# Layer 0's two projections of five chunks by two-by-two blocks with seven products

## The chip, the core and the metric

The kernel runs on one core of a Trainium2 chip. The time is the device time of one execution, in microseconds (us). The engines are TensorE (PE in the profile; PEld are its weight loads), VectorE (DVE), ScalarE (ACT), GpSimd (POOL) and SyncE (SP, here only a queue that issues DMAs). All data are float32. One f32 matmul instruction of the program appears in the profile as two passes, so "x32" in a row of PE means 16 matmuls of the program.

## What is computed

There are 16 sequences of 256 tokens with 256 features, 4096 tokens in all. Layer 0 is a linear recurrence that is gated by a two-layer MLP; layer 1 is causal attention with low-rank keys and values, gated by a linear layer with low-rank experts. Only layer 0 is touched:

```
x  = L0_attn_x
xn = layernorm(x)
s  = recurrence(xn)            # complex diagonal state of 32, plus D * xn
h  = gelu(xn @ proj1.T + b1)   # 256 -> 1024
g  = silu(h @ proj2.T + b2)    # 1024 -> 256
x  = x + s * g
# then layer 1 on x
```

## The kernel before, in words

The tokens are taken in 8 chunks of 512 (two sequences). The program is one list of instructions for each engine. PE's list is the order of the program: a small class, InOrder (line 40), chains each instruction to the one before it. The lists v0 (DVE), a0 (ACT) and g0 (POOL) are chained in the same way where they are used; operations written with nc.vector, nc.scalar or nc.gpsimd are placed by the scheduler. A second class, Later (line 64), keeps instructions back and writes them in portions.

For a chunk of layer 0 the steps are these. norm0 makes layer-norm statistics on DVE (four bn_stats), the power −1/2 on POOL (rs) and the scaled tokens xn on DVE. turn0 turns xn by 8 PE transposes (tp) and copies them out of PSUM to xnT, the first half on ACT, the second on DVE (line 199). hidden (line 655) is the first projection: 8 blocks of 128 hidden rows, each of 2 matmuls with N=512 (rows "ph<-xnT,p1T"), then a GELU on ACT (line 665) into hT. recur (line 680) is the recurrence: 4 matmuls (pb), on DVE a product v and four products w with PSUM operands, on POOL v+w (line 694), on DVE a scan (696), again four products w and hs (699), on POOL the last subtraction (700). mix (line 703), called twice, is the second projection: 256 tokens each time, 16 matmuls with N=256 (rows "pf<-p2T,hT"), a DVE sum with the bias (713) and a Silu on ACT (715). direct (718) is dx = xn * D, two POOL operations (723). outs (726) is four small matmuls (py) and two DVE sums (739). finish0 (741) multiplies by the gate and adds to x, two POOL operations a half.

The chunks 0 and 1 are interleaved by hand at the start, while weights arrive and DVE builds the tables of the recurrence (rot, ct, stb, sns, decay) by doubling columns. In chunks 0 to 3 fold_heads (623) loads and multiplies layer 1's query and output weights of four heads each (psq and pso, four loads on SP, lines 629 to 632), for layer 1. In the last chunk the first steps of layer 1 (norm_begin, transpose_chunk, kv_begin with the row pkv, query_mm) are interleaved. PSUM has three pools: four banks for ph, pb, psq, pso and tp, used in turn as a ring, two for py and two for pf.

Of the kernel before, what the change touches and what calls it, by code (L numbers as in the profile page):

```python
# [18 lines left out]
P = 128  # L19
B, S, D = 16, 256, 256  # L20
NTOK = B * S
CH = 512
# [19 lines left out]
def tile_two_layers(ctx: ExitStack, tc: tile.TileContext, d: dict, out: bass.AP):  # L42
# [192 lines left out]
    def norm_begin(ch):  # L235
        k = chunks[ch]
        st = sm1.tile([P, TPC, 6], F32, tag="ln_st", name=f"st_1_{ch}")
        k.mv = sm1.tile([P, TPC, 2], F32, tag="ln_mv", name=f"mv_1_{ch}")
        v = sm1.tile([P, TPC], F32, tag="ln_ve", name=f"ve_1_{ch}")
        k.rs = sm1.tile([P, TPC], F32, tag="ln_rs", name=f"rs_1_{ch}")  # L240
        for j in range(TPC):
            ve.bn_stats(st[:, j, :], X[ch][:, j, :])
        for j in range(TPC):
            ve.bn_aggr(k.mv[:, j, :], st[:, j, :])
        ve.tensor_scalar(v, k.mv[:, :, 1], LN_EPS, None, ALU.add)
        gp.tensor_tensor(k.rs, v, mhalf, ALU.pow)
# [182 lines left out]
    with ExitStack() as l0:  # L429
# [4 lines left out]
        ps_mm = l0.enter_context(tc.tile_pool(name="ps_mm", bufs=4, space=PSUM))  # L434
        ps_y = l0.enter_context(tc.tile_pool(name="ps_y", bufs=2, space=PSUM))
        ps_f = l0.enter_context(tc.tile_pool(name="ps_f", bufs=2, space=PSUM))
# [186 lines left out]
        def fold_heads(g):  # L623
            hs = slice(g * HG, (g + 1) * HG)
            big = qp.tile([P, 2, HG, D], F32, tag="qg", name=f"wqn_wo{g}")
            small = qm.tile([P, 2, HG, KVL], F32, tag="qmul", name=f"wkb_wvb{g}")
            wqn, wo, wkb, wvb = big[:, 0], big[:, 1], small[:, 0], small[:, 1]

            nc.sync.dma_start(wqn, d["wq_nopeT"][hs].rearrange("h p e -> p h e"))
            nc.sync.dma_start(wkb, d["wkb_T"][:, hs, :])  # L630
            nc.sync.dma_start(wvb, d["wvb_T"][:, hs, :])
            nc.sync.dma_start(
                wo, d["Wo"][g * HG * P : (g + 1) * HG * P, :].rearrange("(h p) e -> p h e", p=P)
            )
            psq = ps_mm.tile([P, 2, HG // 2, 2, KVL], F32, tag="mm", name=f"psq{g}")
            for h in range(HG):
                for c in range(2):
                    pe.matmul(
                        psq[:, c, h // 2, h % 2, :], wqn[:, h, c * P : (c + 1) * P],
                        wkb[:, h, :], start=True, stop=True,  # L640
                    )
            prs = slice(g * HG // 2, (g + 1) * HG // 2)
            nc.vector.tensor_copy(
                wlat[:, :, hs, :], psq.rearrange("p c a b f -> p c (a b) f")
            )
            pso = ps_mm.tile([P, HG // 2, D], F32, tag="mm", name=f"pso{g}")
            for h in range(HG):
                pe.matmul(
                    pso[64 * (h % 2) : 64 * (h % 2) + 64, h // 2, :], wvb[:, h, :],
                    wo[:, h, :], start=True, stop=True,  # L650
                )
            nc.scalar.copy(wout[:, prs, :], pso)


        def hidden(ch, xnT):
            hT = []
            for fc in range(NFC):
                ph = ps_mm.tile([P, CH], F32, tag="mm", name=f"ph_{ch}_{fc}")
                for c in range(2):
# [5 lines left out]
                (a0 if ch == 1 else nc.scalar).activation(  # L665
                    ht, ph, AF.Gelu, bias=b1[:, fc : fc + 1]
                )
# [12 lines left out]
        def recur(ch, xnT):  # L680

            pb = ps_mm.tile([P, S], F32, tag="mm", name=f"pb_{ch}")
            for c in range(2):
                for b in range(2):
                    pe.matmul(
                        pb[64 * b : 64 * b + 64, :], bT[:, c, :],
                        xnT[:, c, b * S : (b + 1) * S], start=(c == 0), stop=(c == 1),
                    )

# [4 lines left out]
            nc.gpsimd.tensor_tensor(v, v, w, ALU.add)  # L694
            g = a2.tile([P, S], F32, tag="g", name=f"g_{ch}")
            nc.vector.tensor_tensor_scan(g, decay, v, 0.0, ALU.mult, ALU.add)
            swapped(w, g)
            h = a2.tile([P, S], F32, tag="hs", name=f"hs_{ch}")
            nc.vector.tensor_tensor(h, g, ct, ALU.mult)
            nc.gpsimd.tensor_tensor(h, h, w, ALU.subtract)  # L700
            return h

        def mix(ch, jp, hT):
            pf = ps_f.tile([P, 2, D], F32, tag="pf", name=f"pf_{ch}_{jp}")
            for j2 in range(2):
                cols = slice((2 * jp + j2) * P, (2 * jp + j2 + 1) * P)
                for fc in range(NFC):
                    pe.matmul(
                        pf[:, j2, :], hT[fc][:, cols], p2T[:, fc, :],
                        start=(fc == 0), stop=(fc == NFC - 1),  # L710
                    )
            zf = a2.tile([P, 2, D], F32, tag="zf", name=f"zf_{ch}_{jp}", bufs=3)
            nc.vector.tensor_tensor(zf, pf, bc(b2_bc, 2), ALU.add)
            if ch:
# [3 lines left out]
        def direct(ch, xn, g=nc.gpsimd):  # L718

            dx = []  # L720
            for b in range(2):
                dx.append(a2.tile([P, 2, D], F32, tag="dx", name=f"dx_{ch}_{b}", bufs=4))
                g.tensor_tensor(dx[b], xn[:, 2 * b : 2 * b + 2, :], bc(d_bc, 2), ALU.mult)
            return dx

        def outs(ch, h, dx):

            py = [
                ps_y.tile([P, 2, D], F32, tag="py", name=f"py_{ch}_{b}") for b in range(2)
# [8 lines left out]
            for b in range(2):  # L738
                nc.vector.tensor_tensor(dx[b], py[b], dx[b], ALU.add)

        def finish0(ch, jp, dx, zf):
            js = slice(2 * jp, 2 * jp + 2)
            nc.gpsimd.tensor_tensor(dx[jp], dx[jp], zf, ALU.mult)
            nc.gpsimd.tensor_tensor(X[ch][:, js, :], X[ch][:, js, :], dx[jp], ALU.add)
# [81 lines left out]
        for ch in range(NCH):  # L826
            last = ch == NCH - 1
            if last:
                place.update(pool=ps_mm, tag="mm")
                norm_begin(0)  # L830
                norm_end(0)
                norm_begin(1)
            if ch > 1:
                hT = hidden(ch, xnT)
            if last:
                transpose_chunk(0)
            if ch == 0:

                zf = [mix(ch, jp, hT) for jp in range(2)]
                turn_b()  # L840
                dx0 = direct(0, xn, g0)
                xn3 = norm0(2)
                hT = hidden(1, xnT2)
                for z in zf:
                    a0.activation(z, z, AF.Silu)
                g = recur(ch, xnT)
                fold_heads(ch)
                h0, zf0 = g, zf
            else:
                if ch == 1:  # L850
                    xn2 = xn3
                elif ch + 1 < NCH:
                    xn2 = norm0(ch + 1)
                g = recur(ch, xnT)
                if ch < NH // HG:
                    fold_heads(ch)
                if ch == 1:
                    zf = mix(ch, 0, hT)
                    outs(0, h0, dx0)
                    for jp in range(2):  # L860
                        finish0(0, jp, dx0, zf0[jp])
                if ch + 1 < NCH:
                    xnT2 = turn0(ch + 1, xn2)
                if last:
                    kv_begin(0)
                    norm_end(1)
                if ch > 1:
                    zf = mix(ch, 0, hT)
                if last:
                    kv_end(0)  # L870
                    router_chunk(0)
                    key_chunk(0)
                if ch == 1:
                    zf = [zf, mix(ch, 1, hT)]
                    dx = direct(ch, xn)
                    outs(ch, g, dx)
                    for jp in range(2):
                        finish0(ch, jp, dx, zf[jp])
                else:
                    dx = direct(ch, xn)  # L880
                    outs(ch, g, dx)
                    if last:
                        query_mm(0, 0)
                        query_mul(0, 0)
                        query_mm(0, 1)
                        query_mul(0, 1)
                        query_rot(0)
                        query_move(0)
                    finish0(ch, 0, dx, zf)
                    zf = mix(ch, 1, hT)  # L890
                    if last:
                        ve.tensor_scalar(bb_bc, bb_bc, 0.5, None, ALU.mult)
                        query_mm(0, 2)
                        query_lat(0, 2)
                        query_mm(0, 3)
                        query_lat(0, 3)
                        query_mm(1, 0)
                        query_mul(1, 0)
                        query_mm(1, 1)
                        query_mul(1, 1)  # L900
                        query_rot(1)
                        query_mm(1, 2)
                        query_lat(1, 2)
                    finish0(ch, 1, dx, zf)
            xn, xnT = xn2, xnT2
# [372 lines left out]
```

## Time and profile before

| what | value |
|---|---|
| median of 3 runs | 946.45 us (945.7 to 947.52) |
| the profiled execution | 946.5 us, of it 944.7 us span |
| mean granted PE clock | 0.998 |
| ph, first projection | 288 passes, 114.2 us in rows |
| pf, second projection | 512 passes, 113.6 us in rows |
| layer 0 | about the first 260 us |

A row "A us, mean ns" gives the busy time of a group of like instructions and the mean of one; the two names before and after "<-" are the target and its sources, and the shapes are partitions x elements. Rows of pipelined matmuls overlap, so the mean of one is longer than the distance from start to start. A chain row names the work, or the wait, that held the end back. In the timeline a row stands for one or several like instructions in a row, with start and duration.

### The profile page before, as it was taken

The page shows a single profiled execution, that of the slowest core. Times are in us where ns is not written, and L with a number is a line of the kernel's source. Part 1 is how long each engine was busy: PE and PEld are TensorE (multiplying, and loading weights), DVE is VectorE, ACT ScalarE, POOL GpSimd, SP SyncE. Part 2 cuts the span into 40 slices and gives each one's busy share as a digit, 9 for nine tenths or more (in the row PEclk, how much of TensorE's full clock was granted, in tenths as well). Part 3 has the DMA queues.
Part 4 walks back from the last instruction along what each step waited for, and adds up shares of the span by engine and source line. Part 5 has one row for each costly group of instructions (what it writes and reads, how often), then busy time and mean ns, then how long its engine had stood idle before and what let it go on. Part 6 is the DMA issues. An engine that isn't in the chain of part 4 may idle for free.

```text
span 944.7 us, 15757 instructions
## 1 busy us (share of the span) xinstructions
PE 928.2 (98%) x4778; PEld 667.7 (71%) x4778; DVE 617.1 (65%) x1943; ACT 427.4 (45%) x1421; POOL 419.0 (44%) x760
## 2 busy tenths in 40 slices
PE   8999999999999899999999999999999999999988
PEld 7765766676676666777677777767777776777776
DVE  6884541343166688867967876796787679677662
ACT  3323223323335646545544564554465455446550
POOL 1327313332145454554554555445464544546450
PEclk9999999999999999999999999999999999999999
DMA  9630000000013777776787777678676767867870
GB/s 282 216 112 1 1 1 0 1 1 1 0 20 60 200 194 188 205 201 172 184 194 187 189 175 206 176 176 208 167 195 170 215 174 171 213 167 186 230 201 29
DMA packets 196597, 133.90 MB, mean 142 GB/s; under 512 B 142304, under 2 KB 187168, under 8 KB 196512
## 3 DMA queue, kind: packets, MB, share of 16 engines
q1 hardware_dynamic: 194192, 128.68, 52.3%
q0 software_dynamic: 1344, 3.67, 1.1%
q8 instruction: 39, 0.64, 0.3%
q10 hardware_dynamic: 976, 0.53, 0.2%
q14 instruction: 46, 0.38, 0.1%
HBM read 63.11 MB, written 52.95 MB: 123 GB/s over the span
## 4 chain that ended last, share of the span: by engine, by line
PE 86%; DVE 7%; POOL 2%; DMA 1%; ACT 1%; SPq 1%; issue 1%; POOLq 0%; ACTq 0%
PE pq L53 22%; PE sc L53 14%; PE po L53 11%; PE ph L53 10%; PE av L53 9%; PE pf L53 9%; PE pg L53 4%; PE pm L53 1%; PE pkv L53 1%; PE tp L53 1%; POOL pr L53 1%; SPq L53 1%; DVE w L53 1%; DMA qg<-qrot 1%; DVE rot L53 1%
## 5 line engine op out<-in xcount | busy, mean ns | idle before, releaser
L53 ACT ACTIVATE pr<-sc,nm 128x256 f32<-128x256 f32 (+7 forms) x512 | 190.0, 381 | 278.5 <-DVE sr L53 196.6
L53 POOL TENSOR_SCALAR pr<-pr,sr 128x256 f32<-128x256 f32 (+7 forms) x512 | 192.6, 395 | 274.6 <-DVE sr L53 256.6
L53 PEld LDWEIGHTS sc<-kT,qg 128*128 128x128 f32 x1024 | 159.5, 191 | 62.7 <-issue 40.3
L53 PE MATMUL sc<-kT,qg 128*128 128x256 f32 (+7 forms) x1024 | 176.5, 306 | 4.9 <-DMA qg<-qrot 3.0
L53 DVE STREAM_TRANSPOSE turned<-pr 128x512 f32<-128x512 f32 x186 | 123.3, 688 | 15.2 <-POOL pr L53 14.4
L53 DVE TENSOR_REDUCE nm<-sc 128x1 f32<-128x256 f32 (+7 forms) x512 | 127.7, 301 | 6.6
L53 PE MATMUL pq<-xnT,wlat 128*128 128x512 f32 x256 | 123.6, 606 | 0.0
L53 PE MATMUL pq<-xnT,wrope 128*128 128x512 f32 x256 | 120.2, 593 | 0.0
L53 PE MATMUL po<-wout,attT 128*128 128x256 f32 x512 | 115.8, 380 | 0.0
L53 PE MATMUL ph<-xnT,p1T 128*128 128x512 f32 (+1 forms) x288 | 114.2, 555 | 1.1 <-DVE xnT L53 0.8
L53 PE MATMUL pf<-p2T,hT 128*128 128x256 f32 x512 | 113.6, 380 | 0.0
L53 PEld LDWEIGHTS po<-wout,attT 128*128 128x128 f32 x512 | 96.4, 190 | 20.9 <-issue 6.4
L53 PEld LDWEIGHTS pf<-p2T,hT 128*128 128x128 f32 x512 | 96.2, 190 | 15.0 <-issue 2.2
L53 ACT ACTIVATION_READ_ACCUMULATOR pr<-sc,nm 128x1 f32 x512 | 103.6, 202 | 0.0
L53 PEld LDWEIGHTS ph<-xnT,p1T 128*128 128x128 f32 x288 | 55.9, 195 | 54.9 <-issue 48.6
L53 PE MATMUL av<-pT,row 128*64 128x256 f32 (+1 forms) x1024 | 90.3, 329 | 0.0
L53 POOL TENSOR_TENSOR qrot<-qmul,qmul 128x512 f32<-128x512 f32 x64 | 82.6, 1311 | 10.4 <-DVE qmul L53 7.0
L53 DVE TENSOR_TENSOR qmul<-pq,rot_q 128x512 f32<-128x512 f32 x128 | 80.9, 674 | 4.9 <-PE pq L53 4.9
L53 DVE TENSOR_TENSOR sc<-sc,kmask 128x96 f32<-128x96 f32 (+1 forms) x192 | 46.0, 240 | 52.2 <-PE sc L53 50.8
L53 PEld LDWEIGHTS av<-pT,row 128*64 128x64 f32 x1024 | 64.0, 137 | 22.6 <-issue 0.5
L53 ACT ACTIVATE qg<-pq 64x512 f32<-64x512 f32 x128 | 75.5, 590 | 4.9 <-PE pq L53 4.1
L53 PEld LDWEIGHTS pq<-xnT,wlat 128*128 128x128 f32 x256 | 46.3, 193 | 32.2 <-issue 32.1
(164 smaller groups left out, 902.9 us busy)
## 6 DMA issues: line engine op xcount, KB each, us to landing
far<-turned SPq DMA_DIRECT2D x248, 192.0 KB, 3.7
pT<-far SPq DMA_DIRECT2D x62, 768.0 KB, 4.7
qg<-qrot SPq DMA_DIRECT2D x256, 64.0 KB, 2.3
x<-in_x_dram SPq DMA_DIRECT2D x7, 512.0 KB, 9.4
out_dram<-o POOLq DMA_DIRECT2D x28, 128.0 KB, 3.3
wqn_wo<-in_wq_nopeT_dram SPq DMA_DIRECT2D x4, 512.0 KB, 4.5
wqn_wo<-in_Wo_dram SPq DMA_DIRECT2D x4, 512.0 KB, 5.3
p2T<-in_proj2T_dram SPq DMA_DIRECT2D x2, 512.0 KB, 7.3
```

Source lines behind the costliest of these rows:

```text
L53: r = getattr(self.engine, name)(*args, **kw)
```

## The change

Chunks 2 to 6 compute both projections by two-by-two blocks with seven block products in place of eight. Chunks 0, 1 and 7 keep the plain method. For a product C = A·B cut into 2x2 blocks, five sums of blocks of the weights, five of the tokens, and sums of the products are needed instead:

- fast_weights1 (five POOL operations of 128x512) and fast_weights2 (four of 128x512 and one of 128x128) make the weight sums once, behind direct of chunks 0 and 1 in POOL's list and ahead of the power of norm0(2).
- fast_tokens makes the five token sums of a chunk on DVE, each 128x256 from two SBUF operands.
- A chunk is done in two steps t, each with half of the hidden rows. hid_a, hid_c and hid_e are the seven products of the first projection, into three PSUM banks r1, r2, r3 with one buffer each; c4 is a copy on ACT, f two DVE sums; a10 and a01 are GELUs from PSUM, a11 and a00 are DVE subtractions from f followed by GELUs (each GELU as two halves of 256).
- sums and sum4 (four POOL operations of 128x512 a step) add the GELU results; out_a, out_b, out_c are the seven products of the second projection of the step before, with N=128, into banks f0 to f3. zf_early, zf_mid, zf_late and zf_last add them, on DVE and (zf_late) on POOL.
- middle writes out the lists of all engines. recur is split: recur_in, and recur_out with a hook between hs and the last subtraction, in which POOL does sum4, finish0 of the second half of two chunks back and the two operations of direct.
- PSUM is given out bank by bank (Ring) in place of three pools.
- mix runs over the hidden blocks outside and the token blocks inside. The second mix of chunk 1 is written in portions into chunk 2 as filler.
- In the last chunk the plain hidden(7) is interleaved with out_a, out_b and out_c of the last step; the loads of fold_heads are issued earlier for groups 2 and 3.

The core of the diff:

```diff
-        ps_mm = l0.enter_context(tc.tile_pool(name="ps_mm", bufs=4, space=PSUM))
-        ps_y = l0.enter_context(tc.tile_pool(name="ps_y", bufs=2, space=PSUM))
-        ps_f = l0.enter_context(tc.tile_pool(name="ps_f", bufs=2, space=PSUM))
+        banks = l0.enter_context(tc.tile_pool(name="ps0", bufs=1, space=PSUM))
...
+        ps_mm = Ring("r1", "r2", "r3", "x")
+        ps_y = Ring("f2", "f3")
+        ps_f = Ring("f0", "f1")
...
+        def recur_out(ch, v, w, ve, ge, between=None):
+
+            ge.tensor_tensor(v, v, w, ALU.add)
             g = a2.tile([P, S], F32, tag="g", name=f"g_{ch}")
-            nc.vector.tensor_tensor_scan(g, decay, v, 0.0, ALU.mult, ALU.add)
+            ve.tensor_tensor_scan(g, decay, v, 0.0, ALU.mult, ALU.add)
             swapped(w, g)
             h = a2.tile([P, S], F32, tag="hs", name=f"hs_{ch}")
-            nc.vector.tensor_tensor(h, g, ct, ALU.mult)
-            nc.gpsimd.tensor_tensor(h, h, w, ALU.subtract)
+            ve.tensor_tensor(h, g, ct, ALU.mult)
+            if between:
+                between()
+            ge.tensor_tensor(h, h, w, ALU.subtract)
...
+        def fast_weights1():
...
+            g.tensor_tensor(fw.w[1], a1(0, 0), a1(1, 1), ALU.add)
+            g.tensor_tensor(fw.w[5], a1(0, 0), a1(0, 1), ALU.add)
+            g.tensor_tensor(fw.w[2], a1(1, 0), a1(1, 1), ALU.add)
+            g.tensor_tensor(fw.w[6], a1(0, 0), a1(1, 0), ALU.subtract)
+            g.tensor_tensor(fw.w[7], a1(1, 1), a1(0, 1), ALU.subtract)
...
+        def fast_tokens(xnT, which):
...
+            for m in which:
+                v0.tensor_tensor(fw.x[m], *how[m])
...
+        def hid_a(t, xnT):
...
+            hid(q, q.r[1], 4, True)
+            hid(q, q.r[0], 3, True)
+            hid(q, q.r[2], 1, True)
...
+            a0.copy(c4, q.r[1])
+            v0.tensor_tensor(fw.f, q.r[0], c4, ALU.add)
+            v0.tensor_tensor(fw.f, fw.f, q.r[2], ALU.add)
...
+        def hid_e(t):
...
+            for n, key in ((1, (1, 1)), (0, (0, 0))):
+                v0.tensor_tensor(q.a[key], fw.f, q.r[n], ALU.subtract)
+                gelu(q, key[1], q.a[key], q.a[key])
...
+        def sums(t):
...
+            g0.tensor_tensor(q.s[1], a[1, 0], a[1, 1], ALU.add)
+            g0.tensor_tensor(a[1, 0], a[0, 0], a[1, 0], ALU.subtract)
+            q.s[3] = a[1, 0]
+            g0.tensor_tensor(q.s[2], q.s[1], a[0, 0], ALU.subtract)
...
+        def middle(ch, xn, xnT, xn2, fill, out1):
...
+            if prev:
+                sums(t - 1)
+            hid_a(t, xnT)
+            out_a(t - 1) if prev else fill.write(8)
+            v, w = recur_in(ch, recur_mm(ch, xnT, X_RING))
+            hid_c(t)
+            out_b(t - 1) if prev else fill.write(4)
+
+            def rest():
+                if prev:
+                    sum4(t - 1)
+                    finish0(ch - 2, 1, out1.dx, out1.z[1], g0)
+                fw.dx[ch] = direct(ch, xn, g0)
+
+            h = recur_out(ch, v, w, v0, g0, rest)
...
+            turn_half(0)
+            hid_e(t)
+            if prev:
+                o = zf_early(ch - 1)
+                out_c(t - 1)
...
+            turn_half(1)
+            if prev:
+                zf_mid(ch - 1, o)
...
+            t += 1
+            if prev:
+                zf_late(ch - 1, o, g0)
+            sums(t - 1)
+            hid_a(t, xnT)
+            if prev:
+                zf_last(ch - 1, o)
+            for z in o.z:
+                a0.activation(z, z, AF.Silu)
+            out_a(t - 1)
...
+            if ch < NCH - 2:
+                fast_tokens(xnT2, (4, 3, 1))
+            outs(ch, h, [dx[:, 2 * b : 2 * b + 2, :] for b in range(2)], v0, XF_RING)
+            hid_c(t)
+            out_b(t - 1)
+            sum4(t - 1)
...
+        dx, dx1 = direct(0, xn, g0), direct(1, xn2, g0)
+        fast_weights1()
+        fast_weights2()
+        xn3 = norm0(2)
+        hT = hidden(1, xnT2, [])
...
+        g = recur(0, xnT)
+        fold_heads(0)
...
+        h1 = recur(1, xnT2)
+        fold_heads(1)
+        xnT = turn0(2, xn3)
+        out1 = Out()
+        out1.z = [mix(1, 0, hT)]
```

## The prediction

> **What bounds the kernel now.** I read the head of the page first, then the chain of waits over layer 0, the timeline of one chunk on VectorE (DVE) and GpSimd (POOL), and the table by stage.
>
> ```profile
> span 944.7 us, 15757 instructions
> PE 928.2 (98%) x4778; PEld 667.7 (71%) x4778; DVE 617.1 (65%) x1943; ACT 427.4 (45%) x1421; POOL 419.0 (44%) x760
> ...
> PE 86%; DVE 7%; POOL 2%; DMA 1%; ACT 1%; SPq 1%; issue 1%; POOLq 0%; ACTq 0%
> ...
> L53 PE MATMUL pf<-p2T,hT 128*128 128x256 f32 x512 | 113.6, 380 | 0.0
> ```
> TensorE (PE) is busy for 98% and is 86% of the chain. The pf row (second projection) never waits: less PE work there is worth its full time, if nothing else becomes late. In chunks 2 to 7 the chain is PE alone:
>
> ```profile
> 178.52 13.73 PE ph L53 x32
> ...
> 194.29 6.91 PE pf L53 x32
> ...
> 202.26 7.10 PE pf L53 x32
> 209.37 13.73 PE ph L53 x32
> ```
> A chunk's period is 209.37 − 178.52 = 30.85 us (33.8 with fold_heads): ph 13.73, pf 14.0, the rest pb, py and transposes. Per pass that is 13.73/32 = 0.429 us at N=512 and 6.91/32 = 0.216 at N=256.
>
> Second, how DVE and POOL share. This is the stretch at the start in which POOL multiplies dx while DVE builds rotation tables from columns of one element:
>
> ```profile
> 30.11 2.50 POOL L53 TENSOR_TENSOR dx<-xn,d_bc 128x512 f32<-128x512 f32 x2
> 30.19 1.21 DVE L53 SCALAR_TENSOR_TENSOR rot<-rot,u 128x1 f32<-128x1 f32 x1
> ...
> 31.44 1.18 DVE L53 TENSOR_TENSOR u<-rot 128x1 f32<-128x1 f32 x1
> ...
> 32.56 2.51 POOL L723 TENSOR_TENSOR dx<-xn,d_bc 128x512 f32<-128x512 f32 x2
> ...
> 32.66 1.20 DVE L53 SCALAR_TENSOR_TENSOR f<-rot,u 128x1 f32<-128x1 f32 x1
> ...
> 35.13 0.16 DVE L53 TENSOR_TENSOR u<-rot 128x1 f32<-128x1 f32 x1
> 35.32 0.22 DVE L53 SCALAR_TENSOR_TENSOR rot<-rot,u 128x1 f32<-128x1 f32 x1
> ```
> Beside POOL's products an operation on one element lasts 1.2 us; when POOL has stopped, at 35.07, it lasts 0.16 to 0.22. DVE gets about one such operation in per POOL operation. POOL can wait too: of two operations of 1.27 each when alone, these two took 2.95, with DVE's two-input g taking 0.89:
>
> ```profile
> 378.31 2.95 POOL L53 TENSOR_TENSOR qrot<-qmul,qmul 128x512 f32<-128x512 f32 x2
> ...
> 379.24 0.89 DVE L53 SCALAR_TENSOR_TENSOR g<-g,h 128x512 f32<-128x512 f32 x1
> ```
> DVE rows that read PSUM, and bn_stats, keep their length beside POOL. The recurrence in a chunk of before runs with POOL idle:
>
> ```profile
> 196.31 0.69 DVE L696 TENSOR_TENSOR_SCAN g<-decay,v 128x256 f32<-128x256 f32 x1
> 197.04 1.71 DVE L53 TENSOR_TENSOR w<-g,sns 32x256 f32<-32x256 f32 x4
> 198.76 0.42 DVE L699 TENSOR_TENSOR hs<-g,ct 128x256 f32<-128x256 f32 x1
> ```
> Last, the price of a PE gap, in the table by stage (busy us of PE, PEld, DVE, ACT and POOL, then granted clock):
>
> ```profile
> 316.00:325.00 9.00, 6.00 (x14) 3.21 (x14) 5.27 (x15) 3.94 (x17) 5.41 (x10) 0.81 0.82 203
> ```
> PE stood 3.16 us and was then granted half its clock for 3.41 us, which costs 1.7. Gaps of 1.7 (355.0) and 2.0 us (909.6) left the clock whole.
>
> **Less PE work.** Chunks 2 to 6 replace 16 block products per projection by 14 half-size ones (seven in each of two steps). First projection: 14 groups of 4 passes at N=256, 14 × 4 × 0.2157 = 12.08, against 13.73: −1.65. Second: 14 groups of 8 passes at N=128. Half of 0.216 would be 0.108; pkv, the nearest row, has 0.112 from start to start (1.87 for 16 with the entry, 0.117). So 14 × 0.893 = 12.51 (13.1 at 0.117) against 13.82: −1.31 (bound −0.7). Together −2.95 a chunk, −14.75 in five. More short groups alternate, at about 0.02 us each: +1.2 in all. Free of waits a chunk takes about 28.1.
>
> **What the other engines take on.** Per chunk POOL goes from 10 us to about 22.3 (14 operations of 128x512 at 1.27, 4 of 128x256 at 0.73, pow 1.02), DVE from 11 to 21, ACT from 10 to 14. None fills 28 us, so on average all of it lies beside PE. Order and the shared access decide.
>
> **Even step of a chunk (3 to 6).** Time from hid_a's first matmul, per-group times as above. hid_a ends 2.6, out_a 5.3, pb 6.4, then hid_c, out_b, half the transposes, hid_e, out_c, the other half: PE is through at 14.5. The next step's hid_a writes bank r2, which has one buffer now; it is free when DVE has made a11 = f − r2. In DVE's written list a11 stands behind scan, four w and hs. recur_in ends at 8.75 (from pb, PSUM operands), POOL's v+w at 9.5. In POOL's list `between` follows directly: sum4, two finish0, two dx, five operations of 128x512 with their inputs ready. DVE's scan, w ×4 and hs all have two SBUF inputs. What I must price is how they pass each other. No row has two-input operations of this size against five POOL operations in a row; the nearest is the first stretch above, one DVE operation per POOL operation. At that, six DVE operations against five of POOL: 5 × 1.16 (what POOL holds of its 1.25) + 0.55 (scan) + 5 × 0.28 = 7.75, so hs ends at 9.53 + 7.75, about 17.4 with its entries, and a11 at 18.1. PE waits 18.1 − 14.5 = 3.6. Bounds: without sharing, 0.69 + 1.71 + 0.42 = 2.8 us, a11 at 12.9, no wait; with all five first, 9.5 + 6.3 + 2.8 + 0.7 = 19.3, a wait of 4.8. I take 3.6, since the near row shows the alternation.
>
> Here a rule of the Trainium skill is weighed: "SBUF — State Buffer", section "Who interferes with whom", says that the port pair of DVE and GpSimd is an exclusive lock, held for the whole instruction, and that a DVE instruction with two SBUF inputs contends with a GpSimd one that reads SBUF. It speaks against this change, which puts most of its additions there. By the rule alone 128x512 and 128x1 operations wait alike and the step stalls 3.6. The qrot row is milder: g lost about 0.2 and POOL 0.45, 0.65 per meeting instead of about 1.2. At 0.65 × 5 the chain ends at 9.5 + 2.8 + 3.3 = 15.6, a11 at 16.3, and the wait is 1.8. But there the engines met once, not five times in a row with all of POOL's inputs ready, so I keep the first value, and 1.8 as the mild case.
>
> **Odd step.** PE work 13.55. sums, zf_late, sum4 and finish0 lie on POOL, fast_tokens (2.1) and xn on DVE, each with PE work of over 2 us between it and its reader. The a01 gelu stands behind two silus and two table loads (2 × 1.28 + 2 × 0.63) and delays hid_e by about 0.5; xn and fast_tokens may push recur_in by up to 1.3. Chunk: 14.54 + 3.65 + 13.55 = 31.74, plus 0.5 to 1.8: 32.2 to 33.5, and a third of 1.7 for a cold clock. Against 30.85 that is +1.4 to +3.2, taken as +2.2: +9 for four chunks (3 to 6). At the mild wait of 1.8: about −0.2 a chunk.
>
> **Chunk 2** has no previous halves to add and plain fillers: −2.6.
>
> **Start.** fast_weights1 and 2 (9 operations of 128x512, one of 128x128) go into POOL's list behind both direct (to 35.07) and ahead of rs_2. They run to 35.0 + 9 × 1.25 = about 46.4. DVE's table chain is then at the same rate as in the first stretch: some 18 operations in 11.4 us, worth 2.7 at 0.15 each, a loss of 8.7. In before DVE runs from the tables through xn (54.48 to 55.86) and recur_in(0) (57.9) without a gap but the 1.1 for rs. So w of pb0 ends at 66.6. psq1 needs pb0's bank (fifth tile in a ring of four): PE, at 59.1, waits till about 66.7; queued behind it stand pso1, turn0(2) and pf. The gap is above 3.16, so half a clock follows (1.7). recur_in(1) comes at 72.3, where the second half of turn0(2) needs pb1's bank; pf(1,0) starts near 73.0 instead of 63.3: **+9.7**. Bounds: 0 if the small operations slip between POOL's (the first row argues against that), 13 if each of DVE's later two-input operations waits too. Weight sums are used only at 90 and later; nobody waits for them.
>
> **Tail.** In chunk 7 the copies of xnT_0 stand on ACT behind z6's table load and two silus; pkv waits about 2.4: +2.4 (0 to 4). SP's DMA issues of fold_load 2 and 3 come earlier in the program; they wait for the buffers of groups 0 and 1 with nothing urgent behind them on SP, and are read 20 us later: nothing. The gelus that out_a and out_c read are ready over 1 us ahead: nothing, what covers them is the pb, hid_c and py work between; each microsecond past it would be PE's own.
>
> **Sum.** 944.7 + 9.7 − 2.6 + 9 + 2.4 = 963.2. The profiled run took 946.5, 1.8 more than its span and level with the median of 946.45; so 965.0 us.
>
> **Rivals.**
> - Sharing is cheap (the other side). If scan to hs takes under 5 us instead of 7.8, a11 comes before 14.5 and the step has no wait; the start's chain then also loses little. 944.7 − 14.75 + 1.2 + 2.4 + 1.8 = 935.4. For it: the qrot rows. Against: 128x1 at 1.2. Chance 0.17, with 932 to 944.
> - Mild: wait 1.8 a chunk, start late as forecast. 965 − 9 − 1 = 955 (945 to 957 with a half-lost start). For it: g's 0.89. Chance 0.23, of it 0.06 within 0.2% of before.
> - Likeliest: 957 to 972. Chance 0.42.
> - Worse: a clock at half after each wait, and recur_in pushed so far that hid_c's gelus are late as well. 965 + 4 × 1.2 + 4 = 974 (972 to 984). For it: the waits of 3.6 lie above the 3.16 that was punished. The rule in "TensorE: Matmul & The Clock Gate", Part 1, has half the clock after a window of about 3.4 us without work; by it 3.6 would be cold only when a window falls into it, by the row above 3.16 was enough once. I price one in three. Chance 0.18.
> - That products at N=128 save nothing (weight loads bind): bounded above, 0.6 a chunk; inside every case.
>
> Range 937 to 975: it leaves out most of the first case's lower half and of the worst. Measurements tell 0.2% (1.9 us) from no change: faster 0.18, same 0.06, slower 0.76.
>
> **What would show it.** Right: a PE gap of about 7 us before psq1 and a granted clock under 1 between 60 and 75; in chunks 3 to 6 one wait of the second hid_a on DVE's a11, 3 to 4 us; scan, w and hs rows near 1.3 us each; POOL rows of 1.5 to 1.8; a period of 32 to 33.5; N=128 passes at 0.112. Wrong: w and hs at 0.42 beside POOL, a period near 28, or the weight sums at 1.25 with the table rows at 0.2.

## The result and the profile after

The changed kernel takes 973.78 us (median of 5, 971.36 to 974.52) against 946.39 for the kernel before: 1.0283 times as long, 95% interval 1.0265 to 1.0300. The forecast was 965.0 in a range of 937 to 975. The profiled execution has a span of 972.0 us, 27.3 more than before. Its page, first the totals, then the chain by engine:

```profile
span 972.0 us, 16726 instructions
...
PE 928.8 (96%) x5138; PEld 704.0 (72%) x5138; DVE 711.7 (73%) x2034; ACT 440.8 (45%) x1476; POOL 486.4 (50%) x814
...
PE 81%; DVE 6%; issue 5%; POOL 4%; ACT 2%; DMA 2%; SPq 1%; POOLq 0%; ACTq 0%
```

PE's busy time did not fall (928.8 against 928.2), although its matmuls are less work: a matmul at half the clock counts as busy for twice as long. In the chain PE fell from 86% to 81%; "issue" (5% after 1%) and POOL (4% after 2%) have taken most of it.

Where the 27.3 us lie is read by comparing PE's start of the same piece of work in both traces (times in us). A piece that the change pushes into the next chunk (out_a to out_c, 7 x 0.893 = 6.25) is counted where it belongs.

| stretch | forecast | measured | from |
|---|---|---|---|
| start, to the second projection of chunk 1 | +9.7 | +11.0 | its first matmul at 74.06; before at 62.04, and 1.0 for chunk 2's transposes, which now stand ahead of it |
| chunk 2 | −2.6 | −3.1 | chunk 3 starts at 115.34 with 6.25 still to do; 113.71 before |
| chunks 3 to 6 | +9 | +15.0 | 115.34 to 256.63, before 113.71 to 240.05 |
| tail, to pkv | +2.4 | +1.9 | pkv at 280.49, before 255.76 |
| layer 1 | 0 | +2.6 | the rest of 27.3 |

**The start.** PE's rows of the timeline around psq of chunk 1 (start, duration, instruction; in brackets the idle time before it):

```profile
58.22 1.03 PE L53 MATMUL pb<-xnT,bT 128*64 128x256 f32 x8
66.82 3.65 PE L53 MATMUL psq<-wkb_wvb,wqn_wo 128*128 128x64 f32 x16 [7.56 <-issue]
70.39 1.98 PE L53 MATMUL pso<-wqn_wo,wkb_wvb 128*64 128x256 f32 x8
72.30 1.97 PE L53 MATMUL tp<-ident,xn 128*128 128x128 f32 x8
```

psq took 2.00 us before and 3.65 here; each row to 74.3 lasts nearly twice as long. psq takes the bank of chunk 0's pb, which DVE reads last in these four products (in before they began at 56.20, 8.8 us earlier):

```profile
64.99 1.72 DVE L53 TENSOR_TENSOR w<-pb,sns 32x256 f32<-32x256 f32 x4
```

They are late because DVE's table chain ahead of them runs like this while POOL makes the weight sums (35.06 to 46.8):

```profile
35.16 1.19 DVE L53 TENSOR_TENSOR u<-rot 128x1 f32<-128x1 f32 x1
36.38 1.18 DVE L53 SCALAR_TENSOR_TENSOR rot<-rot,u 128x1 f32<-128x1 f32 x1
37.49 0.20 DVE L53 TENSOR_SCALAR rot<-rot 128x1 f32<-128x1 f32 x1
37.61 1.18 DVE L53 TENSOR_TENSOR u<-rot 128x1 f32<-128x1 f32 x1
```

**The even step of chunk 3.** DVE, then POOL:

```profile
124.94 1.74 DVE L53 TENSOR_TENSOR_SCAN g<-decay,v 128x256 f32<-128x256 f32 x1 [0.84 <-POOL v L53]
126.71 5.53 DVE L53 TENSOR_TENSOR w<-g,sns 32x256 f32<-32x256 f32 x4
132.26 0.43 DVE L53 TENSOR_TENSOR hs<-g,ct 128x256 f32<-128x256 f32 x1
132.72 0.69 DVE L53 TENSOR_TENSOR a<-misc,r 128x512 f32<-128x512 f32 x1
```
```profile
124.86 1.27 POOL L53 TENSOR_TENSOR a<-a,s 128x512 f32<-128x512 f32 x1
126.09 1.66 POOL L53 TENSOR_TENSOR dx<-dx,zf 128x512 f32<-128x512 f32 x1
127.83 1.33 POOL L53 TENSOR_TENSOR x<-x,dx 128x512 f32<-128x512 f32 x1
129.23 2.73 POOL L53 TENSOR_TENSOR dx<-xn,d_bc 128x512 f32<-128x512 f32 x2
```

Before, the scan took 0.69 and the four w 1.71 (0.43 each). Here it is 1.74 and 5.53 (1.4 each) beside POOL's five, and hs, which comes when POOL has finished, is at 0.43. POOL itself is hardly slowed: one of its five takes 1.66, the others 1.27 to 1.37. hs ends at 132.69, 17.35 us after the step's start at 115.34. PE, which was through at 130.0, starts when a11 (the row a<-misc,r) is there:

```profile
129.39 0.60 PE L53 MATMUL tp<-ident,xn 128*128 128x128 f32 x4
133.46 3.78 PE L53 MATMUL r<-x,p1T 128*128 128x256 f32 x8 [3.48 <-DVE a L53]
```

From start to start that is 4.07 us where 0.43 would do, an excess of 3.64 us, and it is the same in each of chunks 3 to 6. And the row of 8 passes lasts 3.78 us in place of 1.99: half a clock once more.

### The profile page after: what moved, and what is told of

Same layout as the page of the kernel before. It is cut to its first block, busy times and chain, and to the rows that moved or that the text cites. A ratio compares the mean times of both kernels' runs of the same rounds, so it can differ in the third digit from the quotient of the medians.

```text
span 972.0 us, 16726 instructions
## 1 busy us (share of the span) xinstructions
PE 928.8 (96%) x5138; PEld 704.0 (72%) x5138; DVE 711.7 (73%) x2034; ACT 440.8 (45%) x1476; POOL 486.4 (50%) x814
## 4 chain that ended last, share of the span: by engine, by line
PE 81%; DVE 6%; issue 5%; POOL 4%; ACT 2%; DMA 2%; SPq 1%; POOLq 0%; ACTq 0%
PE pq L53 22%; PE sc L53 14%; PE po L53 10%; PE av L53 9%; PE ph L53 5%; PE pg L53 4%; PE pf L53 4%; PE r L53 4%; DVE w L53 2%; PE f L53 2%; PE pm L53 2%; PE pkv L53 1%; POOL s L53 1%; PE tp L53 1%; DVE g L53 1%
## 5 line engine op out<-in xcount | busy, mean ns | idle before, releaser
L53 PEld LDWEIGHTS pq<-xnT,wrope 128*128 128x128 f32 x256 | 45.7, 191 | 32.4 <-issue 32.1
L53 POOL TENSOR_TENSOR rs<-ve,mhalf 128x4 f32<-128x4 f32 (+1 forms) x17 | 16.7, 984 | 65.6 <-DVE ve L53 51.7
L53 PE MATMUL ph<-xnT,p1T 128*128 128x256 f32 (+1 forms) x128 | 44.9, 508 | 0.8 <-DVE xnT L53 0.8
L53 DVE TENSOR_TENSOR o<-po,g 128x256 f32<-128x256 f32 x32 | 13.5, 423 | 42.1 <-PE po L53 42.0
```

What stands on the lines that cost most here:

```text
L53: r = getattr(self.engine, name)(*args, **kw)
```

## The experiments

Theory A, that of the forecast: DVE's operations that need the access to SBUF that it shares with POOL pass POOL's one for one, and the change has put five POOL operations next to DVE's recurrence chain and ten next to its table chain; PE's waits follow from that, and half a clock from the waits. Theory B: POOL and DVE are too full for the additional sums wherever they stand.

**1. The five operations of `between` ahead of v+w.** POOL had stood idle there for 7.77 us.

```diff
-            h = recur_out(ch, v, w, v0, g0, rest)
+            rest()
+            h = recur_out(ch, v, w, v0, g0)
```

> The five POOL operations of `between` (sum4, two of finish0, two of direct) stand ahead of v+w in POOL's list in place of behind it. Theory A (DVE's scan, w x4 and hs alternate with them, one for one): scan 0.69, w 0.43, hs 0.42 with POOL idle, the wait of 3.5 us ahead of the odd step's hid_a is gone in chunks 3 to 6 and with it the half clock that follows each (4 x 3.64 of wait and 9.2 of clock): 973.8 - 23.8 = 950, the period of chunks 5 and 6 from 34.0 to about 28.7. Theory B (DVE's list is too long and a11 late wherever POOL's operations stand): above 968, the wait stays over 2.5 us.

Measured: 953.21 us, 1.0066 of before (1.0051 to 1.0081), 20.6 below the changed kernel. DVE in the same step:

```profile
126.52 0.69 DVE L53 TENSOR_TENSOR_SCAN g<-decay,v 128x256 f32<-128x256 f32 x1 [2.29 <-POOL v L53]
127.24 1.71 DVE L53 TENSOR_TENSOR w<-g,sns 32x256 f32<-32x256 f32 x4
128.96 0.43 DVE L53 TENSOR_TENSOR hs<-g,ct 128x256 f32<-128x256 f32 x1
```

The chain is back at 2.8 us. Of the wait of 3.64, 0.2 is left in chunks 3 and 4, and no half clock follows in any of the four. In chunks 5 and 6 two waits of 0.56 and 0.78 came in its place. The first is ahead of hid_c: POOL, now earlier, runs beside xn's four operations (5.32 us there), and the sums f behind xn keep a PSUM bank. The second is ahead of the odd step: v+w now stands in POOL's list behind the five. The period of chunks 5 and 6 is 30.0 us rather than the 28.7 that was expected.

**2. Half a dose.** sum4 and the two of finish0 ahead, the two of direct behind v+w.

```diff
             def rest():
-                if prev:
-                    sum4(t - 1)
-                    finish0(ch - 2, 1, out1.dx, out1.z[1], g0)
                 fw.dx[ch] = direct(ch, xn, g0)
 
+            if prev:
+                sum4(t - 1)
+                finish0(ch - 2, 1, out1.dx, out1.z[1], g0)
             h = recur_out(ch, v, w, v0, g0, rest)
```

> Half a dose: of the five POOL operations of `between`, sum4 and the two of finish0 stand ahead of v+w, only the two of direct stay behind it. Theory A (each POOL operation there costs DVE's chain one hold of 1.16 us): the chain scan to hs is 2.8 + 2 x 1.16 = 5.1 us, a11 comes 15.3 us after the step's start, the wait is 0.8 us in place of 3.6, and no half clock follows: 973.8 - 4 x 2.8 - 9.2 = 953.4. Theory B (any POOL work beside the chain makes its six DVE operations last 1.4 each): the wait stays over 3 us, above 968.

Measured: 955.66 us, 1.0100 (1.0087 to 1.0113). The wait ahead of the odd step is 0.70 us in chunks 3 and 4 and 1.23 in 5 and 6, where the 0.56 of experiment 1 lies ahead of it. The wait follows the number of POOL operations behind v+w: 3.64 at five, 0.70 at two, 0.2 at none (chunks 3 and 4).

**3. The weight sums later.** Five behind the recurrence of chunk 1, the others ahead of chunk 2's v+w.

```diff
-        fast_weights1()
-        fast_weights2()
         xn3 = norm0(2)
...
         h1 = recur(1, xnT2)
+        fast_weights1()
         fold_heads(1)
...
         xn, xn2 = xn3, norm0(3, end0)
+        fast_weights2()
```

> The weight sums are made later on POOL: the five of the first projection behind the recurrence of chunk 1, the five of the second ahead of chunk 2's v+w; all else as in the changed kernel. Theory A (beside them DVE's table chain crawls): the rotation tables are ready about 8.5 us earlier, PE's wait of 7.5 us ahead of the second psq goes, and the half clock with it (8 us at half, 4 us): about 963. Theory B (the sums cost the same wherever they stand, since DVE meets them anyway): 971 or more.

Measured: 971.75 us, 1.0267 (1.0250 to 1.0284), what theory B said. But the trace shows both halves of an exchange. psq of chunk 1 runs at 59.64 and the second projection at 64.52 instead of 74.06: the cause at the start is right. What was won was lost in chunk 2, as POOL's rows show:

```profile
83.86 1.27 POOL L53 TENSOR_TENSOR x<-x,dx 128x512 f32<-128x512 f32 x1
85.08 1.27 POOL L53 TENSOR_TENSOR t<-p2T 128x512 f32<-128x512 f32 x1
...
90.22 0.46 POOL L53 TENSOR_TENSOR misc<-b_bc 128x128 f32<-128x128 f32 x1
90.63 0.73 POOL L53 TENSOR_TENSOR v<-v,w 128x256 f32<-128x256 f32 x1
```

v+w has had its operands since 83.9 and stands in POOL's list behind five weight sums until 90.6. PE then waits 6.8 us ahead of the odd step of chunk 2, and the clock is at half from 93.1 to 99.9, in part during that wait.

**4. Both moves.**

> Both moves together. Theory A: 973.8 - 23.8 - 10.8 = 939, so faster than before (946.4). Theory B: above 965. If the two waits hide each other, between 945 and 955.

Measured: 954.94 us, 1.0088 (1.0063 to 1.0113), the middle case: no gain over the first experiment alone, since the same wait (7.3 us here) is in chunk 2. That the time lies in the band that was expected for two waits hiding each other is chance: they did not.

**5. PE kept busy in its waits.** 33 matmuls that nobody reads ahead of the second psq, 15 ahead of the odd steps' hid_a in chunks 3 to 6, into banks that are free there; the waits stay.

```diff
+        def keep_warm(tag, n, name):
+            ps = banks.tile([P, CH], F32, tag=tag, name=name)
+            for z in range(n):
+                pe.matmul(ps[:, 0:P], ident, ident, start=True, stop=True)
```

> The changed kernel with additional matmuls that nobody reads, in PE's waits: 33 of N=128 ahead of the second psq, 15 ahead of the odd step's hid_a in chunks 3 to 6. The waits themselves stay. If the half clock after the waits is a loss of its own (4.0 at the start, 9.2 in four chunks by the clock rows), the granted clock stays at 1 and the time is about 961. If the clock is a sign only and the waits are all of the loss: 974.

Measured: 963.68 us, 1.0176 (1.0161 to 1.0191), 10.1 below the changed kernel. From the table by stage, chunks 3 to 6 (busy us of PE, PEld, DVE, ACT and POOL, granted clock); first this kernel, then the changed one:

```profile
120.00:260.00 140.00, 137.92 (x940) 121.56 (x939) 116.58 (x190) 53.47 (x101) 95.96 (x82) 1.00 0.00 1
```
```profile
120.00:260.00 140.00, 124.71 (x772) 107.98 (x772) 109.18 (x176) 50.84 (x97) 87.47 (x75) 0.93 0.00 1
```

In chunks 3 to 6 the clock is whole and the waits are as long as before; PE is 8.9 us faster there, of the 9.2 that the clock rows said. At the start only 1.0 of 4.0 came back (from psq to pf 6.3 us in place of 7.2), because a wait for the next bank took the place of the half clock:

```profile
71.84 0.63 PE L53 MATMUL tp<-ident,xn 128*128 128x128 f32 x4 [2.25 <-DVE w L53]
```

So 10 us of the 27 are the clock's own.

**6. Which operations pass one for one.** Both layers are left out. Eight DVE operations of a kind are started together with six POOL additions of 128x512.

> Both layers are left out; the time means nothing, the rows do. Eight DVE operations of one kind are started together with six POOL additions of 128x512 from SBUF: additions of two SBUF operands, of PSUM and SBUF, a tensor_scalar with scalars from a column, one with a constant, bn_stats, a scan, an addition on 128x1; a last phase has one POOL addition. Theory A (two-operand or column-scalar reads from SBUF pass POOL one for one): the first six of twosb, ptr, scan and tiny at 1.2 to 1.4 us, the others at 0.34 to 0.42 as alone, POOL at 1.5 to 1.6 in the former and 1.25 in the latter. Theory B (one meeting costs 0.65 as in the qrot row): twosb at about 0.6 and POOL near 1.6.

From one run, in which only the rows count. The groups of the trace (line, engine, operation, tiles, shapes, count, then busy us and mean ns of one):

```profile
L84 DVE TENSOR_TENSOR_SCAN d_scan<-go_scan 128x256 f32<-128x256 f32 x8 | 9.5, 1182 | 5.0 <-ACT go_scan L65 4.8
L68 POOL TENSOR_TENSOR pl_scan<-go_scan 128x512 f32<-128x512 f32 x6 | 7.9, 1321 | 2.2 <-ACT go_scan L65 1.8
L78 DVE TENSOR_TENSOR d_twosb<-go_twosb 128x256 f32<-128x256 f32 x8 | 7.7, 964 | 1.4 <-ACT go_twosb L65 1.1
L82 DVE TENSOR_SCALAR d_imm<-go_imm 128x256 f32<-128x256 f32 x8 | 7.0, 877 | 1.9 <-ACT go_imm L65 1.6
L68 POOL TENSOR_TENSOR pl_psumsb<-go_psumsb 128x512 f32<-128x512 f32 x6 | 6.2, 1040 | 3.3 <-ACT go_psumsb L65 2.9
L79 DVE TENSOR_TENSOR d_psumsb<-gps_psumsb,go_psumsb 128x256 f32<-128x256 f32 x8 | 3.4, 424 | 2.2 <-ACT go_psumsb L65 2.0
```

An operation with one operand in PSUM is not touched (424 ns), nor is bn_stats (428). The means of the others hide two kinds: beside POOL each of six rows of two SBUF operands lasts 1.14 us, of the scan 1.35, of a column-scalar tensor_scalar 1.08; the two outside last 0.42, 0.69 and 0.41. POOL's rows are 1.10 and 1.30 beside the first two, and not the 1.5 to 1.6 that was expected: it is DVE that waits. That is the forecast's alternation; the 0.6 for DVE and 1.6 for POOL of theory B did not come. POOL's addition reads one tile twice here and is shorter than in the kernel (1.04 alone against 1.27), and DVE's row is shorter with it: 1.14 beside 1.10 here, 1.4 beside 1.3 in the even step.

**7. Both moves, the weight sums in POOL's free stretches.** `between` stands ahead of v+w as in experiment 1 (in chunk 2 behind the recurrence). Experiments 8 to 10 each build on the one before. One sum between the two recurrences, four behind, three ahead of finish0 of chunk 0, the rest behind chunk 2's recurrence.

```diff
         g = recur(0, xnT)
+        fwl.write(1)
         fold_heads(0)
         h1 = recur(1, xnT2)
+        fwl.write(4)
         fold_heads(1)
...
             outs(0, g, dx)
+            fwl.write(3)
             finish0(0, 0, dx, zf[0], g0)
```

> As the run with `between` ahead of v+w, and the weight sums in POOL's free stretches: one between the recurrences of chunks 0 and 1, four behind the latter, three ahead of finish0 of chunk 0, the rest in chunk 2 behind its recurrence together with finish0's second half and direct. Theory A: the start costs nothing more than before, 953.2 - 10.9 = 942.3, so 0.4% faster than before. Theory B (these sums collide wherever they are): 950 or more.

Measured: 948.40 us, 1.0020 (1.0010 to 1.0030); 6 more than theory A's and below theory B's 950. Three sums now run beside xn of chunk 3 (three operations in 4.04 us), and f behind it is late. So hid_c of chunk 2 waits 3.7 us, and the clock is at half for 6.8 us from 82.3 on.

**8. xn on ACT, and the GELU table loaded early.**

```diff
+                    a0.activation(
+                        xn[:, j, :], src[:, j, :], AF.Identity,
+                        bias=nb[:, j : j + 1], scale=rs[:, j : j + 1],
+                    )
...
                 a0.activation(z, z, AF.Silu)
+            tiny = sm.tile([P, 1], F32, tag="tiny", name=f"tiny_{ch}")
+            a0.activation(tiny, b1[:, 0:1], AF.Gelu)
```

> As the run before, with two more edits: the scaled tokens xn of chunks 4 to 6 and 7 come from ACT (four operations behind c4 of the next chunk) in place of four DVE operations with column scalars, and a GELU of one column behind the two silus loads the table before a10 is ready. Theory A: the waits of 0.76 and 0.78 in chunks 5 and 6 and of 0.5 in each chunk go: 942.3 - 3.1 - 2.5 = 936.7. If ACT becomes late: 942 or more.

Measured: 950.04 us, 1.0029 (1.0019 to 1.0040): no gain over experiment 7. The waits of 0.5 and 0.56 did go. But chunks 5 and 6 became earlier than POOL's list, and v+w, with operands since 179.8, stands behind it (POOL's rows):

```profile
178.31 1.27 POOL L53 TENSOR_TENSOR dx<-dx,zf 128x512 f32<-128x512 f32 x1
179.65 1.28 POOL L53 TENSOR_TENSOR x<-x,dx 128x512 f32<-128x512 f32 x1
181.01 2.50 POOL L53 TENSOR_TENSOR dx<-xn,d_bc 128x512 f32<-128x512 f32 x2
183.46 0.73 POOL L53 TENSOR_TENSOR v<-v,w 128x256 f32<-128x256 f32 x1
```

PE waited 2.3 and 2.0 us for a11 there, from POOL's order this time.

**9. direct behind the recurrence, chunk 3's xn on ACT too.** The edit is against the changed kernel, the lines of experiments 7 and 8 left out.

```diff
+                sum4(t - 1)
+                finish0(ch - 2, 1, out1.dx, out1.z[1], g0)
...
+            h = recur_out(ch, v, w, v0, g0)
...
+            fw.dx[ch] = direct(ch, xn, g0)
```

> As the run with xn on ACT, with POOL's list thinned ahead of v+w: only sum4 and the two of finish0 stand before it, direct's two behind the recurrence's last subtraction, where POOL stood idle for 2.5 us; xn of chunk 3 is made by ACT too. Theory A (what remains late is only POOL's place in line): the waits of 2.3 and 2.0 us ahead of the odd step in chunks 5 and 6 and of 3.9 at the first hid_c of chunk 2 go, with the half clock behind them (3.4 + 1.7): 950.0 - 8.2 - 5 = 936.8, faster than before by 1.0%. Theory B (POOL and DVE together are too full for the seven products, whatever the order): 944 or more.

Measured: 938.68 us, 0.9901 of before (0.9880 to 0.9921), 1.0% faster than the kernel before. The table by stage for chunks 4 and 5:

```profile
136.14:164.18 28.04, 28.04 (x195) 25.45 (x193) 20.81 (x43) 15.40 (x30) 19.57 (x20) 1.00 0.00 1
164.18:192.11 27.93, 27.93 (x194) 25.34 (x193) 21.12 (x43) 14.85 (x30) 22.36 (x22) 1.00 0.01 1
```

PE has no gap, and a chunk takes 28.0 us against 30.85: with nothing waiting the change is worth 2.9 us a chunk, as costed. Theory B, that POOL and DVE are too full wherever the sums stand, is refuted by this.

**10. The tail.** As experiment 9, with chunk 6's two silus behind the copies of layer 1's turned tokens on ACT.

```diff
+        norm_begin(1)
+        transpose_chunk(0)
         for z in z6.z:
             a0.activation(z, z, AF.Silu)
-        norm_begin(1)
-        transpose_chunk(0)
```

> As the run before, with the two silus of chunk 6 behind the copies of layer 1's first turned tokens on ACT. By the forecast's tail term PE's wait of 2.1 us ahead of pkv goes: 2 us below the run before, 934.8. If the wait has another cause (the copies late for themselves): the same as the run before.

Measured: 938.84 us, 0.9910 (0.9892 to 0.9928), not told apart from experiment 9. The cause of the wait was right: ahead of pkv it is gone. But PE then waits 2.3 us ahead of pk, for DVE, and half a clock follows. The gain went into the next wait.

## Why the prediction was right, and where it was not

The forecast was 18.5 us more, and 27.3 were measured. The 8.8 us between them are, rounded, the start (1.3), chunk 2 (−0.5), chunks 3 to 6 (6.0), the tail (−0.5) and layer 1 (2.6). The direction and the three places of loss were forecast with their mechanism. That the time lies within the range is in part luck: it is 1.2 us below the upper end, and at the 974 of the case called "Worse", which had a chance of 0.18. Of that case one half came, a half clock after each wait, and at a higher price; the other, late GELUs of hid_c, did not.

**Less PE work: right.** Eight passes of N=128 start every 0.111 us (0.89 for a group of eight). Without their waits, the loss by the clock and fold_heads, chunks 3 to 6 take 28.1 to 28.3 us (chunk 5: 33.96 − 3.64 − 0.51 − 1.7), and experiment 9 measures 28.0 directly; the forecast said 28.1.

**The even step: right in mechanism and size.** From the scan to the end of hs it is 7.75 us, the very sum of the forecast; hs ends 17.35 after the start (forecast 17.4), and PE waits 3.64 (3.6). The sign that POOL's rows would last 1.5 to 1.8 held for one of five: DVE waits, POOL hardly. Experiments 1 and 2 show that the POOL operations behind v+w are the cause, and experiment 6 the passing one by one. The choice of the 128x1 row over the milder qrot row was right; why that row was mild was not tried. Nor was a11's own place varied: it stands behind hs in DVE's list, and the bank that it frees has one buffer; by the program's order PE's wait needs both.

**The start: right in mechanism, a little small.** The wait was 7.56 (forecast 7.6). Experiment 3 shows its cause. The half clock lasted 8.0 us from the wait's end in place of 3.41, a loss of 4.0 in place of 1.7. Some of this was hidden: with the clock whole PE would have waited for pb1's bank, as experiment 5 shows (2.25 us). What is left, 1.0 us, is most of the 1.3 between +9.7 and +11.0.

**The odd step: partly right.** The GELU behind two silus and two table loads costs 0.51 (forecast 0.5), and in experiment 8, which loads the table early, it is gone. The allowance of up to 1.3 us for xn and fast_tokens was not used in the changed kernel, probably since its waits left POOL time; it came in experiment 1, as 0.56 and 0.78.

**The clock: the step that was mis-sized.** The forecast took "a third of 1.7 for a cold clock" per chunk, 2.3 us in four. It came after each of the four waits, and twice for two stretches of 3.41 us: a loss of 3.1, 2.7, 1.7 and 1.7, 9.2 us in all. These 6.9 us more than priced, less the unused allowance of the odd steps, are the 6 us by which chunks 3 to 6 were missed. The records of the granted clock show why. In every trace they change only at multiples of 3.413 us from one another, a grid that lies differently in each run. In stretches of that grid the table for the changed kernel (chunk 4), and then for experiment 3, reads (PE's busy time is the first number behind the comma, the granted clock the third from the end):

```profile
166.95:170.36 3.41, 1.34 (x13) 1.10 (x11) 3.38 (x3) 0.00 (x0) 3.25 (x3) 1.00 0.00 0
170.36:173.78 3.42, 2.01 (x5) 1.64 (x6) 3.33 (x8) 1.97 (x5) 0.72 (x1) 0.50 0.00 0
173.78:177.19 3.41, 3.41 (x10) 2.65 (x9) 1.53 (x3) 2.04 (x3) 2.81 (x4) 0.50 0.02 5
```
```profile
164.74:168.15 3.41, 1.82 (x17) 1.58 (x15) 3.38 (x3) 0.00 (x0) 3.33 (x3) 1.00 0.00 0
168.15:171.57 3.42, 1.54 (x7) 1.38 (x8) 3.34 (x7) 1.50 (x4) 1.12 (x2) 1.00 0.00 0
171.57:174.98 3.41, 3.41 (x28) 3.25 (x27) 3.24 (x8) 2.73 (x5) 2.42 (x3) 1.00 0.02 5
```

The wait is the same 3.64 us. Above, a stretch with PE busy for 1.34 of 3.41 us is followed by half the clock. Below, the grid splits the wait evenly, 1.59 and 1.88 us idle, and the clock stays whole. Counted over the eleven traces of the whole kernel from 14 us on, for stretches at full clock: with PE idle for 1.0 to 1.4 us, none of 45 was followed by half; 1.4 to 1.9, 9 of 27; 1.9 and more, 25 of 25. So a stretch wholly without work, the rule that the prediction weighed, is not needed. A wait of 3.64 lies across the grid so that both parts stay under 1.9 only for 0.16 us of 3.41, which makes its half clock nearly sure (0.95, an estimate from these counts). "One in three" was too low: of the prediction's three gaps two were short ones, and the longest had been followed by half a clock. Once the clock is at half, less is enough: with 0.6 us idle or more the next stretch was at half as well in 13 of 13, with less in 3 of 37. That is the second stretch of chunks 3 and 4, where 0.64 and 1.41 us of the wait fell into the first; in chunks 5 and 6 nothing did. The three exceptions are all at the start, in a stretch of psq and pso without a gap; why was not tried. Experiment 5 confirms the size: 8.9 us back in the four chunks without touching a wait.

**Tail: right** (1.9 us of wait, forecast 2.4). **Layer 1: missed.** It was taken as unchanged and took 2.6 us more. The clock is not the reason in this trace, for before and after have one stretch at half there. About 1.2 us were lost by its first scores, where PE waits 1.28 for ACT's qg at 313.5, and 1.4 near the end, with waits of 1.16 and 0.38 between 929 and 934. In all ten changed traces layer 1 takes 2.5 to 6.9 us longer from pkv to the last matmul. What makes these operations late was not tried.

**Rivals.** That sharing is cheap is refuted for this kernel by experiments 1, 2 and 6. That the change can still make the kernel faster, near the rival's 935, is shown by experiment 9 (938.7), but by moving the sums away from DVE's chain, not because meetings are cheap.

## What to carry to other kernels

Count not only an engine's load but which DVE operation stands beside which POOL operation: one with two SBUF operands took nearly as long as the POOL operation beside it (1.4 us in place of 0.43), one with a PSUM operand paid nothing (0.42). Put additional POOL work where the other side reads PSUM, and look what stands behind it in POOL's own list: v+w was late there in experiments 1, 3, 4 and 8. Price a PE wait of about 3.6 us at 1.7 us extra at the least, and up to 3.1; one of 2 us can go either way, since the grid may cut it in two.

## What was not expected of the hardware

A tensor_scalar with a constant, one operand in SBUF, passes POOL one for one too: 1.08 us beside it, 0.29 alone. An addition on 128x1 gets in twice per POOL operation (0.16 and 0.89). The half clock is decided by idle time inside a fixed grid of 3.413 us, somewhere from 1.4 to 1.9 us of it, not by a whole stretch without work.
